# Adding the branches' results in accumulating transfers, and scaling two of three norms on VectorE, in a deformable-convolution block

## The chip, the core and the metric

The kernel runs on one core of one Trainium2 chip. The metric is the device time of one execution in microseconds (us). Three executions of the kernel before took 6637.6, 6637.77 and 6625.94 us; the median is 6637.6 us. Differences below some 0.2% (13 us) are not told from no change.

The engines are named as in the profile: PE is TensorE's matrix multiply and PEld its weight load, DVE is VectorE, ACT is ScalarE, POOL is GpSimd, SP is SyncE, which issues most of the transfers (DMAs). Each engine works through its own queue in order, and engines wait for one another by semaphores.

## What is computed

The input x is (2, 256, 128, 128) in fp32. Two layers follow each other: `x = x + layer0(groupnorm(x))`, then `x = x + layer1(groupnorm(x))`. Layer 1 is a 3x3 convolution with ternary weights and is not touched here. Layer 0 is this:

```python
def _branch(x, w_off, w_def, lw, lb, pad, dil):
    off = _conv(x, w_off, pad, dil)
    y = _deform_dw(x, off, w_def, pad, dil)       # 9 bilinear samples a pixel, depthwise
    return jax.nn.gelu(_ln2d(y, lw, lb), approximate=False)

x1 = _branch(x, off_w1, def_w1, bw1, bb1, 1, 1)
x2 = _branch(x, off_w2, def_w2, bw2, bb2, 9, 9)
x3 = _branch(x, off_w3, def_w3, bw3, bb3, 12, 12)
c = jnp.einsum('bchw,oc->bohw', x, conv_w[:, :, 0, 0]) + conv_b[None, :, None, None]
out = _ln2d(x1 + x2 + x3 + c, n1_w, n1_b)
h = out.transpose(0, 2, 3, 1)
h = jax.nn.gelu(h @ mlp_w1.T + mlp_b1, approximate=False) @ mlp_w2.T + mlp_b2
out = _ln2d(h.transpose(0, 3, 1, 2) + out, n2_w, n2_b)
```

`_ln2d` normalises each pixel over its 256 channels. There are three such norms on the way: the first in each of the three branches, with a Gelu behind it; the second over the sum of the branches; the third behind the MLP. The second and third have no function behind them.

## The kernel before

The kernel has three stages, one after the other. Stage A (to about 910 us) computes the offsets of all three branches and writes tables of x and of the samples' weights ("hats") to HBM. Stage B (to about 5830 us) takes the samples and runs all the rest of layer 0. Stage C is layer 1. The change lies in stage B alone.

**Sampling.** `sample_near` walks over 2 images x 66 row tiles x 3 branches, 396 units. For a unit, SP loads the hats `hy` and `hx` (line 1347, three buffers each) and table tiles `xs` (L1326), DVE multiplies the hats into a matrix `A` (L1367), PE multiplies it with the table tiles into PSUM `pm` (L1468, four buffers), ACT evicts `pm` into `ev` (L1480 and L1488, three buffers), and DVE adds `ev`, weighted per channel, into rings of rows (L1429, the first of a row by ACT at L1411). So each unit goes DVE, PE, ACT, DVE.

**The tail.** Four image rows (512 pixels) make a group; there are 64 groups, each in three branches, 192 chains. Once a branch's four rows are complete in its ring, its chain begins: `PixelTail.branch`, a generator. It yields a number of steps to pause; `Tail.advance` makes one step and lets every chain that is due emit its next instructions. Sampling calls `advance` twice for each unit and each half of the channels, some 1,580 times in all. So the tail's instructions are laid between those of the sampling by the count of steps, and the order on every engine is the order of emission. A yield has up to three values: the pause in steps; how many buffers the chain holds from then on; and whether the next piece is heavy for ACT (`True`: of the chains due with this mark, one goes on in a step). Buffers `v`, `other`, `xn`, `S`, `hT`, `xr` come from one pool of nine (`VBUFS`), of 512 KB each, and a chain is held back when the buffers would not do (`Tail.may`). At most four chains may be within a norm (`NORMS`).

A chain does this:

- All three branches: PE turns the ring's pixels into rows (L905, L913), ACT copies them into `v` (L921). `moments`: DVE takes mean and variance of each of four rows of 128x256 (L1101, L1103), adds a constant (L1105, L1106), POOL raises to the power -0.5 and multiplies (L1107, L1108) into `rs`. After seven steps `scaled` makes four ACTIVATEs on ACT (L1115), each `func(scale * row + bias)` in place, two in one step and two in the next; here with Gelu.
- Branch 0 then stores `v` to HBM, `g12d` (L1179, from SP). Branch 1 loads that into a second tile `other` (L1186), adds on DVE (L1189) and stores the sum (L1191). Branch 2 loads that (L1186), adds it on DVE (L1198), and goes on alone.
- Branch 2 loads x (`xn`), subtracts a mean on ACT (L1202), multiplies on PE by the 1x1 convolution's weights and adds on DVE (L1145). Second norm: `moments`, seven steps, `scaled` with Identity (L1115 again). Then PE turns the rows back (L1154), ACT copies into `S` (L1221), the MLP follows (matmuls L890 and L1137, Gelu L1230, addition L1145). Third norm: `moments`, seven steps, `scaled` with Identity. Turned back once more (L1154), DVE scales and adds x (L1254) and takes statistics for layer 1 (L1258), and SP stores the result (L1260).

All transfers of the chain are issued by SP, in the same queue as the loads of hats and tables. A DMA that waits for an engine keeps those behind it in that queue waiting too.

Of the kernel before, what the change touches and what calls it, by code (L numbers as in the profile page):

```python
# [13 lines left out]
AF = mybir.ActivationFunctionType  # L14
ALU = mybir.AluOpType
# [56 lines left out]
def conv_preact_kernel(ctx: ExitStack, tc: tile.TileContext, t: dict, out: bass.AP):  # L72
    nc = tc.nc
# [634 lines left out]
    with ExitStack() as actx:  # L708
        psum = actx.enter_context(tc.tile_pool(name="ps_a", bufs=1, space=PSUM))

        def gps():
# [4 lines left out]
        k = {  # L716
            "dxs": dxs,
            "zero": ap.tile([P, C], F32, name="zero"),
            "wz": ap.tile([P, KC, NZ], F32, name="wz"),
            "shift": ap.tile([P, len(dxs), P], F32, name="shift"),  # L720
            "mid": ap.tile([P, ZG, NOFF], F32, name="mid"),
            "hatw": ap.tile([P, 2, NTAP * NH], BF16, name="hatw"),
            "parts": [ap.tile([P, 2, ZG, P], BF16, name=f"parts{i}") for i in range(3)],
            "zr": ap.tile([P, ZRING, NZ], F32, name="zr"),
# [110 lines left out]
    class Tail:  # L835
# [135 lines left out]
        def branch(self, b, br, g, y):  # L971

            pin = self.pin
            cols = slice(g * NG, (g + 1) * NG)
            gv = g12d[b].rearrange("(k p) f -> p k f", p=P)[:, :, cols]
            z = []
            yield from self.normalised(z, y, (b, br, g))
            v = z[0]
            for c in range(KC):
                pin(  # L980
                    nc.scalar.activation(
                        v[:, c, :], z[1 + c], AF.Gelu,
                        scale=bw[:, br, c : c + 1], bias=bb[:, br, c : c + 1],
                    )
                )
            if br == 0:
                yield 2
                nc.sync.dma_start(gv, v)
                self.stored.add((b, br, g))
                return  # L990
            yield 1, 1 + br
            other = self.tile("other")
            while (b, br - 1, g) not in self.stored:
                yield 1
            nc.sync.dma_start(other, gv)
            if br == 1:
                yield 2
                pin(nc.vector.tensor_tensor(v, v, other, ALU.add))
                yield 2
                nc.sync.dma_start(gv, v)  # L1000
                self.stored.add((b, br, g))
                return
            xn = self.tile("xn")
            nc.sync.dma_start(xn, x[b].rearrange("(k p) h w -> p k (h w)", p=P)[:, :, cols])
            yield 4
            for c in range(KC):
                pin(
                    nc.scalar.activation(
                        xn[:, c, :], xn[:, c, :], AF.Identity, bias=negmean[b][:, c : c + 1]
                    )  # L1010
                )
            yield 1
            yield from self.finish(b, g, v, other, xn)
# [75 lines left out]
    class PixelTail(Tail):  # L1089
# [70 lines left out]
        def branch(self, b, br, g, y):  # L1160

            pin = self.pin
            gv = g12d[b].rearrange("c f -> (c f)").rearrange("(g p e) -> g p e", p=P, e=KC * NG)[g]
            xv = x[b].rearrange("(k p) h w -> p k (h w)", p=P)[:, :, g * NG : (g + 1) * NG]
            yield from self.entered()
            yield 0, 1, True
            v = self.tile("v")
            vf = v.rearrange("p k n -> p (k n)")
            vv = vf.rearrange("p (j c) -> p j c", c=C)
            rows = [vv[:, j, :] for j in range(NG // P)]  # L1170
            self.turned(vv, y, (b, br, g))
            self.read.add((b, br, g))
            rs = self.moments(rows)
            yield 7, min(1 + br, 2), True
            yield from self.scaled(rows, rs, AF.Gelu)
            self.norms -= 1
            if br == 0:
                yield 2
                nc.sync.dma_start(gv, vf)  # L1179
                self.stored.add((b, br, g))  # L1180
                return
            other = self.tile("other")
            of = other.rearrange("p k n -> p (k n)")
            while (b, br - 1, g) not in self.stored:
                yield 1
            nc.sync.dma_start(of, gv)  # L1186
            if br == 1:
                yield 2
                pin(nc.vector.tensor_tensor(vf, vf, of, ALU.add))  # L1189
                yield 2  # L1190
                nc.sync.dma_start(gv, vf)  # L1191
                self.stored.add((b, br, g))
                return
            yield 1, 3
            xn = self.tile("xn")
            nc.sync.dma_start(xn, xv)
            yield 2
            pin(nc.vector.tensor_tensor(vf, vf, of, ALU.add))  # L1198
            yield 2, 2, True
            for c in range(KC):  # L1200
                pin(
                    nc.scalar.activation(  # L1202
                        xn[:, c, :], xn[:, c, :], AF.Identity, bias=negmean[b][:, c : c + 1]
                    )
                )
            yield 1
            pairs = [(xn[:, c, :], convs[b][:, c, :]) for c in range(KC)]
            adds = [self.product("pc1", vv, convb3, pairs, h) for h in range(2)]
            yield 1, 1
            for add in adds:  # L1210
                add()
            yield 2
            yield from self.entered()
            rs = self.moments(rows)
            yield 7, None, True
            yield from self.scaled(rows, rs, AF.Identity)
            self.norms -= 1
            yield 2, 2, True
            S = self.tile("S")
            for c in range(KC):  # L1220
                pin(nc.scalar.copy(S[:, c, :], self.channels(rows, c)))  # L1221
            yield 1, 3
            hT = []
            for m in range(MC):
                if m % KC == 0:
                    hT.append(self.tile("hT"))
                hp = self.bank("hp")
                self.matmul(hp, [(w1[:, c, m * P : (m + 1) * P], S[:, c, :]) for c in range(KC)])
                pin(
                    nc.scalar.activation(  # L1230
                        hT[-1][:, m % KC, :], hp, AF.Gelu, bias=b1[:, m : m + 1]
                    )
                )
                yield 1, 4 if m < MC - 1 else 3
            pairs = [(hT[m // KC][:, m % KC, :], w2[:, m, :]) for m in range(MC)]
            add = self.product("h2", vv, b23, pairs, 0)
            yield 1, 3
            add()
            add = self.product("h2", vv, b23, pairs, 1)
            yield 1, 1  # L1240
            add()
            yield 2, 2
            yield from self.entered()
            rs = self.moments(rows)
            xr = self.tile("xr")
            nc.sync.dma_start(xr, xv)
            yield 7, None, True
            yield from self.scaled(rows, rs, AF.Identity)
            self.norms -= 1
            yield 2  # L1250
            for c in range(KC):
                zc = self.channels(rows, c)
                pin(
                    nc.vector.scalar_tensor_tensor(  # L1254
                        xr[:, c, :], zc, n2w[:, c : c + 1], xr[:, c, :], ALU.mult, ALU.add
                    )
                )
                pin(nc.vector.bn_stats(stats2[b][:, c, g, :], xr[:, c, :]))  # L1258
            yield 2, 1
            nc.sync.dma_start(  # L1260
                x1d[b].rearrange("(k p) f -> p k f", p=P)[:, :, g * NG : (g + 1) * NG], xr
            )
# [365 lines left out]
    with cmp.Else():  # L1628
        with ExitStack() as bctx:
            psum = bctx.enter_context(tc.tile_pool(name="ps_b", bufs=1, space=PSUM))  # L1630
            pool = bctx.enter_context(tc.tile_pool(name="bpool", bufs=1))
            k = {
                "A": [pool.tile([PX, 9, RI, WA], F32, name=f"A{i}") for i in range(2)],
            }
# [356 lines left out]
```

## Time and profile before

| what | value |
|---|---|
| median of three runs | 6637.6 us |
| the profiled execution | 6632.7 us, its span 6630.8 us |
| instructions in the trace | 100591 |
| PE busy | 6275.4 us, 95% of the span |
| PEld busy | 4993.0 us, 75% |
| DVE busy | 5906.2 us, 89% |
| ACT busy | 4189.3 us, 63% |
| POOL busy | 686.7 us, 10% |
| moved by DMA | 1360.49 MB, mean 205 GB/s |

"Busy" is the time in which at least one instruction of the engine runs. Instructions of one engine overlap at their ends, so a group's mean duration is longer than the time from one start to the next. A busy PE is not a PE at its peak. The costliest groups of stage B before, as the page has them: L1468 matmuls 3248.5 us for 17424 instructions, L1429 2481.2 us for 6372, L1480 1987.5 us for 4488, L1367 1009.5 us for 1124, L1107 on POOL 472.0 us for 320.

### The profile page before, as it was taken

The numbers are of one execution on the slowest core, as the hardware profiler recorded it, in microseconds if no ns is written. First come the engines' busy times: TensorE is split into PE (matmuls) and PEld (weight loads), VectorE is DVE, ScalarE is ACT, GpSimd is POOL, SyncE is SP. The second block draws the span as 40 slices with busy tenths as digits, with TensorE's granted clock in tenths as the row PEclk, the third lists the DMA queues.
The fourth block names the chain that finished last, engine by engine and source line by source line (L and its number), as shares of the span: only waits on it lengthen the run. The fifth ranks groups of instructions, "written<-read, shape, count | busy, mean of one in ns | idle before, by whom it ended". The sixth has DMA issues, their size and how long they took to land.

```text
span 6630.8 us, 100591 instructions
## 1 busy us (share of the span) xinstructions
PE 6275.4 (95%) x32242; PEld 4993.0 (75%) x32242; DVE 5906.2 (89%) x13772; ACT 4189.3 (63%) x8690; POOL 686.7 (10%) x665
## 2 busy tenths in 40 slices
PE   6899978999999999999999999999999999989999
PEld 3455558888888888888888888888888888734444
DVE  8766668999999999999778999999999999689996
ACT  2344447777777777777676777777777777554442
POOL 0000000111111111111110111111111111200000
PEclk9999978999999999999999999999999999989999
DMA  8976667877787777787667877788777777343332
GB/s 290 274 214 199 201 169 216 226 217 219 223 225 217 223 217 224 222 222 206 181 194 203 227 219 219 221 223 227 223 217 220 215 222 209 122 164 132 139 139 90
DMA packets 635795, 1360.49 MB, mean 205 GB/s; under 512 B 109592, under 2 KB 290344, under 8 KB 618736
## 3 DMA queue, kind: packets, MB, share of 16 engines
q1 hardware_dynamic: 617328, 1318.97, 68.9%
q10 hardware_dynamic: 17408, 33.56, 1.6%
q8 instruction: 261, 4.28, 0.3%
q14 instruction: 286, 2.34, 0.1%
q0 software_dynamic: 512, 1.34, 0.1%
HBM read 1087.10 MB, written 266.47 MB: 204 GB/s over the span
## 4 chain that ended last, share of the span: by engine, by line
PE 53%; DVE 30%; DMA 8%; ACT 5%; issue 3%; SPq 0%; POOL 0%; DVEq 0%; ACTq 0%; POOLq 0%
PE pm L1468 22%; DVE ring L1429 13%; PE pc L1810 6%; PE hp L890 6%; PE h L1137 5%; DVE A L1367 5%; PE pz L364 4%; DMA hx<-hats 3%; PE pc L1137 3%; DMA xa<-in_x 3%; ACT ev L1480 2%; ACT v L1115 2%; DVE st L1101 1%; PE ph L463 1%; PE tp L905 1%
## 5 line engine op out<-in xcount | busy, mean ns | idle before, releaser
L1468 PE MATMUL pm<-A,xs 96*128 96x216 f32 (+2 forms) x17424 | 3248.5, 343 | 176.4 <-ACT ev L1480 45.4
L1468 PEld LDWEIGHTS pm<-A,xs 96*128 96x128 f32 x17424 | 3049.1, 195 | 374.1 <-ACT ev L1480 119.2
L1429 DVE SCALAR_TENSOR_TENSOR ring<-ev,defw,ring 128x256 f32<-128x256 f32 (+4 forms) x6372 | 2481.2, 451 | 98.1 <-ACT ev L1480 47.8
L1480 ACT COPY ev<-pm 128x432 f32<-128x432 f32 (+4 forms) x4488 | 1987.5, 483 | 869.3 <-PE pm L1468 695.8
L1367 DVE TENSOR_TENSOR A<-hy,hx 96x768 f32<-96x768 f32 (+1 forms) x1124 | 1009.5, 945 | 164.1 <-DMA hx<-hats 89.8
L1107 POOL TENSOR_TENSOR rs<-rs,mhalf 128x4 f32<-128x4 f32 x320 | 472.0, 1475 | 4202.5 <-DVE rs L1106 3543.9
L1810 PE MATMUL pc<-cring,signs 128*128 128x512 bf16 x3456 | 757.9, 382 | 17.0 <-ACT cring L1727 7.4
L1115 ACT ACTIVATE v<-v,rs 128x256 f32<-128x256 f32 x1280 | 694.4, 594 | 16.7 <-POOL rs L1108 16.6
L1810 PEld LDWEIGHTS <-signs 128*128 128x128 bf16 x3456 | 339.6, 98 | 434.6 <-issue 27.7
L890 PE MATMUL hp<-S,w 128*128 128x512 f32 x1024 | 493.9, 607 | 0.8 <-ACT S L1221 0.8
L364 PE MATMUL pz<-wz,xa 128*128 128x486 f32 x1024 | 461.6, 578 | 25.3 <-DVE zr L371 25.3
L1137 PE MATMUL h<-w,hT 128*128 128x256 f32 x2048 | 477.1, 379 | 0.0
L1101 DVE BATCH_NORM_STATS2 st<-v 128x6 f32<-128x256 f32 x1280 | 446.9, 410 | 30.8 <-ACT v L921 30.8
L1411 ACT ACTIVATE ring<-ev,defw 128x256 f32<-128x256 f32 (+1 forms) x856 | 404.5, 485 | 24.2
L1137 PEld LDWEIGHTS h<-w,hT 128*128 128x128 f32 x2048 | 369.3, 190 | 65.5 <-issue 1.0
L364 PEld LDWEIGHTS pz<-wz,xa 128*128 128x128 f32 x1024 | 189.2, 191 | 189.3 <-issue 126.1
L921 ACT COPY v<-tp 128x512 f32<-128x512 f32 x384 | 207.8, 598 | 182.7 <-PE tp L913 182.4
L1230 ACT ACTIVATE hT<-hp,b 128x512 f32<-128x512 f32 x256 | 176.1, 688 | 218.6 <-PE hp L890 214.6
L890 PEld LDWEIGHTS hp<-S,w 128*128 128x128 f32 x1024 | 196.7, 197 | 139.4 <-issue 121.3
L470 ACT ACTIVATE hb<-ph 96x512 f32<-96x512 f32 (+1 forms) x384 | 209.8, 596 | 144.2 <-PE ph L463 135.6
L1137 PE MATMUL pc<-convw,xn 128*128 128x256 f32 x1024 | 271.1, 393 | 2.4 <-ACT xn L1202 2.4
L371 ACT COPY zr<-pz 128x486 f32<-128x486 f32 x128 | 72.1, 564 | 256.5 <-PE pz L364 253.8
(246 smaller groups left out, 5132.5 us busy)
## 6 DMA issues: line engine op xcount, KB each, us to landing
hy<-hats SPq DMA_DIRECT2D x1112, 288.0 KB
hx<-hats SPq DMA_DIRECT2D x1112, 288.0 KB
xs<-tables SPq DMA_DIRECT2D x1452, 96.0 KB
g12d<-v SPq DMA_DIRECT2D x128, 512.0 KB
other<-g12d SPq DMA_DIRECT2D x128, 512.0 KB
hats<-hb SPq DMA_DIRECT2D x64, 720.0 KB
hats<-hb SPq DMA_DIRECT2D x64, 576.0 KB
xa<-in_x ACTq DMA_DIRECT2D x64, 512.0 KB
```

The lines of the kernel that those rows point to most:

```text
L364: nc.tensor.matmul(pz[:, 0:NZ], lhsT=xt[:, c, r, :], rhs=k["wz"][:, c, :], start=c == 0, stop=c == KC - 1,)
L890: nc.tensor.matmul(out, lhsT=w, rhs=v, start=i == 0, stop=i == n - 1)
L1101: pin(nc.vector.bn_stats(st[:, j, :], rows[j]))
L1107: nc.gpsimd.tensor_tensor(rs[:, 0, :], rs[:, 0, :], mhalf[:, 0:n], ALU.pow)
L1115: nc.scalar.activation(row, row, func, scale=rs[:, 0, j : j + 1], bias=rs[:, 1, j : j + 1])
L1137: nc.tensor.matmul(bank[:, j, :], lhsT=v[:, px], rhs=w, start=False, stop=i == len(pairs) - 1,)
L1367: nc.vector.tensor_tensor(dst, hy[:, i0:i1].rearrange("p i t w -> p t i w"), hx[:, i0:i1].rearrange("p i t w -> p t i w"), ALU.mult,)
L1411: pin(nc.scalar.mul(dst, src, w))
L1429: pin(nc.vector.scalar_tensor_tensor(dst, src, w, dst, ALU.mult, ALU.add))
L1468: nc.tensor.matmul(pv[:, j, :, m0:m1, :], lhsT=xts[b, Rt][t][:, c * P : (c + 1) * P], rhs=A[:, y0:y1, m0:m1, AO + t * CI : AO + (t + 1) * CI],
L1480: nc.scalar.copy(dst.rearrange("p m (t j) -> p t m j", j=CI), pm[:, 0 : len(ts), 0:n].rearrange("p t (m j) -> p t m j", j=CI),)
L1810: nc.tensor.matmul(pc, lhsT=signs[:, k, (h * 3 + t) * 3 + kx, m * P : (m + 1) * P], rhs=xc[:, i, k, t * JC : (t + 1) * JC, kx : kx + W], s ...
```

## The change

Branch 1 no longer loads, adds and stores: it issues one transfer from POOL that adds `v` to what lies in HBM. Branch 2 issues one transfer from POOL that adds what lies in HBM to `v` in SBUF. The two DVE additions, the tile `other` and its loads are gone. The first norm keeps its ACTIVATEs with Gelu; the four ACTIVATEs of the second and of the third norm become four `tensor_scalar` on DVE (multiply by one value for each pixel, add another), in one step and without the mark for ACT. The pauses and the numbers of held buffers are set accordingly.

```diff
             rs = self.moments(rows)
-            yield 7, min(1 + br, 2), True
+            yield 7, 1, True
             yield from self.scaled(rows, rs, AF.Gelu)
             self.norms -= 1
...
-            other = self.tile("other")
-            of = other.rearrange("p k n -> p (k n)")
             while (b, br - 1, g) not in self.stored:
                 yield 1
-            nc.sync.dma_start(of, gv)
             if br == 1:
-                yield 2
-                pin(nc.vector.tensor_tensor(vf, vf, of, ALU.add))
-                yield 2
-                nc.sync.dma_start(gv, vf)
+                nc.gpsimd.dma_start(gv, vf, accum_op=ALU.add)
                 self.stored.add((b, br, g))
                 return
-            yield 1, 3
+            nc.gpsimd.dma_start(vf, gv, accum_op=ALU.add)
+            yield 1, 2
             xn = self.tile("xn")
             nc.sync.dma_start(xn, xv)
-            yield 2
-            pin(nc.vector.tensor_tensor(vf, vf, of, ALU.add))
-            yield 2, 2, True
+            yield 4, 2, True
...
             rs = self.moments(rows)
-            yield 7, None, True
-            yield from self.scaled(rows, rs, AF.Identity)
+            yield 7
+            for j, row in enumerate(rows):
+                pin(
+                    nc.vector.tensor_scalar(
+                        row, row, rs[:, 0, j : j + 1], rs[:, 1, j : j + 1], ALU.mult, ALU.add
+                    )
+                )
             self.norms -= 1
```

The last hunk stands twice, for the second and for the third norm.

More of the change, by code (lines that the diff above doesn't have):

```diff
@@ L1246, in branch @@
             nc.sync.dma_start(xr, xv)
-            yield 7, None, True
-            yield from self.scaled(rows, rs, AF.Identity)
+            yield 7
+            for j, row in enumerate(rows):
+                pin(
+                    nc.vector.tensor_scalar(
+                        row, row, rs[:, 0, j : j + 1], rs[:, 1, j : j + 1], ALU.mult, ALU.add
+                    )
+                )
             self.norms -= 1
```

## The prediction

> **What bounds the kernel now.** I read the slices first, then the chain of waits, then the waits and windows of the middle stage, last the groups that the diff touches.
>
> ```profile
> PE   6899978999999999999999999999999999989999
> DVE  8766668999999999999778999999999999689996
> ACT  2344447777777777777676777777777777554442
> DMA  8976667877787777787667877788777777343332
> PE 53%; DVE 30%; DMA 8%; ACT 5%; issue 3%; SPq 0%; POOL 0%; DVEq 0%; ACTq 0%; POOLq 0%
> ```
>
> Rows of digits: one slice is 166 us; last row: the chain that ended last, by engine. The change lies in slices 6 to 34, where the samples are taken (the first L1468 matmul starts at 920 us, the last L1429 ends at 5704 us: 4785 us). There PE and DVE are both at 9, ACT at 7. The windows, columns PE, weight loads, DVE, ACT, POOL, then clock, DMA share and GB/s:
>
> ```profile
> 2000.00:2500.00 500.00, 489.61 (x2590) 433.93 (x2589) 479.11 (x1215) 364.55 (x797) 68.58 (x67) 0.99 0.79 220
> 4000.00:4500.00 500.00, 489.73 (x2614) 434.38 (x2614) 484.36 (x1232) 365.59 (x801) 73.18 (x68) 1.00 0.80 223
> ```
>
> PE works 98% of the time, DVE 96%, ACT 73%. So two engines bound the stage by turns, with 2 to 4% between them. The chain of waits, followed through the stage, gives the turns: PE about 2530 us, DVE 1470 (31%), ACT 320, DMA 320. A turn of ACT looks like this (start, length, what):
>
> ```profile
> 2052.81 0.52 ACT ev L1480
> 2053.32 0.99 ACT v L1115 x2
> 2054.31 1.25 ACT ev L1480 x3
> ...
> 2056.29 0.98 ACT v L1115 x2
> 2057.27 1.05 ACT ev L1480 x3
> 2058.32 1.00 ACT v L1115 x2
> 2059.32 0.41 ACT ev L1480
> ```
>
> The reader is to see that the norms' scalings (L1115) stand in front of the evictions L1480 for which PE waits: pairs of ACTIVATE of 0.99 us delay PE by as much.
>
> [...] the 128x1024 additions took 1.22 us, the 120x1536 tensor_scalar L474 0.95. [...] The trace has no accumulating transfer.
>
> **The change part by part.** The built order of instructions shows it done as told: 128 accumulating DMAs on POOL, 256 fewer DMAs on SP, two DVE additions per group gone, 512 tensor_scalars in, 512 ACTIVATEs out; the MLP's matmuls come one step (5 to 17 L1468 matmuls) earlier, the order is otherwise kept. I price from these rows (group: busy us, mean ns; then starts on DVE):
>
> ```profile
> L1115 ACT ACTIVATE v<-v,rs 128x256 f32<-128x256 f32 x1280 | 694.4, 594 | 16.7 <-POOL rs L1108 16.6
> L1189 DVE TENSOR_TENSOR v<-v,other 128x1024 f32<-128x1024 f32 x64 | 77.9, 1218 | 2.0 <-DMA other<-g12d 1.9 <-issue 0.2
> L1198 DVE TENSOR_TENSOR v<-v,other 128x1024 f32<-128x1024 f32 x64 | 77.7, 1214 | 0.0
> L251 DVE TENSOR_SCALAR dn<-wk,q_pr,q_nc 128x256 f32<-128x256 f32 x18 | 7.3, 406 | 0.1
> ...
> 104.24 0.40 DVE L249 TENSOR_SCALAR sg<-wk,q_pr,q_er 128x256 bf16<-128x256 f32 x1
> 104.56 0.41 DVE L251 TENSOR_SCALAR dn<-wk,q_pr,q_nc 128x256 f32<-128x256 f32 x1
> 104.89 0.60 DVE L423 COPY offs<-po 128x432 f32<-128x432 f32 x1
> ```
>
> *Additions out (DVE).* Neighbours overlap, so I count from start to start: the addition at 2010.85 us is followed at 2011.98, 1.13 us. 128 x 1.13 = 145 us off DVE. The chain's pieces for L1189 and L1198 sum to 11 + 15 = 26 us; so 26 on the path.
>
> *Scalings in (DVE).* L251 is the same form with two pointer scalars: 0.41 us, and 0.325 from start to start (104.24, 104.56, 104.89). 512 x 0.325 = 166 us; if none overlap 512 x 0.406 = 208. DVE is on the path for 31% of the stage, so 166 x 0.31 = 51 us on the path. Bounds: half of it (26) if DVE's 4% idle takes the rest; 208 if DVE became the bound throughout. Net DVE load: +21 us (to +63).
>
> *Scalings out (ACT).* 0.99 us for two: 512 x 0.495 = 253 us off ACT. The chain holds 110 us of L1115 in this stage; by number 512 of 1280 are those that go (44 us); matching the pieces with the program's order gives 64. I take 64. Bounds: 0 if PE has no more to give, since its idle time in the stage that names ACT is 45 + 42 + 33 = 120 us (L1480, the S copies L1221, L1488); 120 if all of that goes.
>
> *Wait of the scaling.* It waits on DVE for POOL's rs, and behind it stand the L1429 that PE's buffers wait for. Moments are issued seven steps ahead: some 1,580 steps in 4785 us are 3.0 us each, so 21 us. From L1106 to the end of L1108 it took 2.7 us (median), 6.3 at most. Margin 15 us: nothing.
>
> *Transfers.* SP loses 192 issues net of the 64 first stores: 128 loads (0.53 us) and 64 stores (0.33), 89 us of issue, and the wait that stood in its queue:
>
> ```profile
> SPq L1191 <- DVE v L1189: 389.1, 60, 13.5
> SPq L1186 <- PE h L1137: 147.2, 29, 6.9
> DVE A L1367 <- DMA hx<-hats: 89.8, 54, 13.3
> ```
>
> Behind these queue the hats and tables; but most hats wait for DVE's builds (L1367) anyway, issued after L1189, and only 23 us of the chain are SP's own. I take 5 us. POOL gets 128 issues and, in front of later rs, the wait for the Gelu and for the earlier transfer. The nearest row, an indirect DMA of POOL, took 0.95 us: 128 us on an engine that is 14% busy; hidden by the 15 us margin. Bytes: before 256 transfers of 512 KB (134 MB, 13% of 220 GB/s x 4785 us); after 64 plain and 128 accumulating. At the price of a plain transfer each, 25% less of 13%; at twice[...], 25% more: DMA load -3% to +3%, on 320 us of DMA turns about 10 us either way. I take 0. The result is needed seven steps (21 us) after its issue, against 4.0 to 9.6 us to landing of POOL's transfers here.
>
> *Buffers.* The second tile (other) is no longer held, so chains may start earlier; gain 0 to 10, I take 0. The drain after 5705 us is PE-bound (110 of 125 us busy) and its matmul order is unchanged: 0.
>
> **Sum.** Taken off the path 26 + 64 + 5 = 95; of removed pieces I count 0.8, since another engine's turn is close behind (76); added 51. Result -25 us. The profiled execution took 6632.7 us (span 6630.8 and 1.9 around): 6608. The median of the runs is 4.9 above it: 6613 us.
>
> **Rivals.**
> 1. *More than that* (0.12): ACT's bursts were what kept PE from running ahead, and with them all 120 us of PE's waits for ACT and the full DVE removal come: about -90, 6548. For: ACT's pairs sit between evictions. Against: ACT waits 696 us for PE at L1480; it is often idle first.
> 2. *Hidden* (0.17): PE at 98% has nothing to give, the DVE work nearly cancels (+21 us x 0.31 = 7): 6638 to 6645.
> 3. *VectorE becomes the bound* (0.13, the slower side): each scaling takes 0.41 us without overlap[...], and DVE's net +63 us counts nearly in full, while ACT's relief buys nothing: +30 to +63, about 6690. It decides once DVE's idle in the steady windows falls from 4% to under 2% with PE's rising.
> 4. *Accumulating transfers cost a multiple* (0.08): at four times a plain one, 64 + 512 = 576 units against 256, DMA share 0.79 to 0.95; the hats come late, and 320 us of DMA turns grow by half: +100 to +160, 6760.
>
> That the change does something else is ruled out by the built order.
>
> **How the numbers follow.** The forecast has 0.50 (own range 6575 to 6628), the rivals 0.12, 0.17, 0.13 and 0.08. A measurement here tells no less than 0.2% (13 us) from no change. Faster by more: 0.50 + 0.12 less 0.02 for the forecast's near edge = 0.60; within: 0.17, some of rival 2's upper end lost and the edge gained, 0.18; slower: 0.22. The range leaves out half of rival 1 (0.06), rival 4 (0.08) and the upper end of rival 3 (0.05): 6560 to 6685.
>
> **What would show it.** ACT's share in windows 2000 to 2500 falls from 73% to about 68%; DVE's stays at 96 to 97%; tensor_scalar rows of 0.40 us, 512 of them; no wait of DVE for POOL above a few us; L1115 on the chain falls from 2% to about 1%. Wrong if scalings last over 0.5 us, if DVE waits for the accumulating transfers at L1145, or if the DMA share rises above 0.85.

## The result, and the profile after

The changed kernel took 7035.8 us, median of five runs (7021.75 to 7042.38), against 6637.8 us for the kernel before (five runs): 1.0599 times as long, 95% interval 1.0585 to 1.0613. The forecast was 6613 us, faster by 0.4%. Its profiled execution has a span of 7034.0 us.

From the page of the changed kernel, the slices (here one is 176 us):

```profile
PE   5899978899999999999998999999999999879999
...
DVE  7866668888898888888768888888988988679997
ACT  2344456666666666666556666666666666535443
...
DMA  8966678777777777777558777777777777433332
```

VectorE, ScalarE and the DMA engines each lose about a tenth in the middle stage, TensorE keeps its nine. Only GpSimd became busier, with 12% of the span in place of 10%; so none of them became the bound. The windows of the same kernel, with the columns of the windows before (PE, weight loads, DVE, ACT, POOL, clock, DMA share, GB/s), give the amount:

```profile
2000.00:2500.00 500.00, 466.28 (x2400) 411.68 (x2399) 447.28 (x1159) 322.39 (x690) 83.09 (x72) 0.96 0.75 197
4500.00:5000.00 500.00, 465.62 (x2392) 409.97 (x2391) 441.54 (x1144) 318.93 (x681) 84.40 (x73) 0.97 0.74 197
```

TensorE fell from 98% to 93%, VectorE from 96% to 89%, and the granted clock from 0.99 or 1.00 to 0.96 or 0.97. Two engines that both idle more may be waiting for each other. The table of waits, TensorE's rows first and VectorE's next, names where:

```profile
PE zc L1154 <- DVE v L1248: 242.2, 63, 5.9
...
PE zc L1154 <- issue: 60.8, 27, 5.4
...
PE zc L1154 <- PE pm L1471: 14.7, 22, 1.0
...
DVE A L1370 <- PE pm L1471: 370.7, 67, 8.5
```

Columns: who waits, on which line, for whom, then us in total, times, longest. (Line numbers below the change move by a few from kernel to kernel: L1468 of before is L1471 here, L1367 is L1370, L1429 is L1432. L1248 and L1211 are the new scalings of the third and the second norm; L1154, the transposes behind both, keeps its number.) The same two places in the kernel before, from its groups and its waits:

```profile
L1154 PE MATMUL zc<-ident,v 128*128 128x128 f32 x1024 | 141.0, 280 | 12.4 <-ACT v L1115 10.0 <-DVE st L1101 2.3
...
DVE A L1367 <- PE pm L1468: 72.9, 55, 4.6
```

TensorE waits 318 us ahead of the transposes; before, it was 12.4 us. VectorE writes each `A` into one of two buffers and waits until TensorE has read what stood there; this wait grew from 72.9 to 370.7 us. So TensorE's standstill comes back to VectorE.

One such wait, in the timeline of the changed kernel (start, length, engine, what; in brackets the idle time before it):

```profile
2629.79 10.81 PE L1471 MATMUL pm<-A,xs 96*128 96x216 f32 x59
...
2636.45 2.69 DVE L1370 TENSOR_TENSOR A<-hy,hx 96x768 f32<-96x768 f32 x3
...
2639.07 3.12 DVE L1432 SCALAR_TENSOR_TENSOR ring<-ev,defw,ring 128x256 f32<-128x256 f32 x8
...
2642.11 1.40 DVE L1101 BATCH_NORM_STATS2 st<-v 128x6 f32<-128x256 f32 x4
...
2644.04 1.38 DVE L1248 TENSOR_SCALAR v<-v,rs 128x256 f32<-128x256 f32 x4
...
2644.59 2.21 PE L1154 MATMUL zc<-ident,v 128*128 128x128 f32 x8 [4.00 <-DVE v L1248]
```

TensorE ends its matmuls at 2640.6 and comes to the transposes. The scalings that they need stand on VectorE behind work that was emitted ahead of them, and start 3.4 us later. Nothing is wrong with the scalings: `rs` is there (VectorE's idle time ahead of L1248 is 0.2 us in all, none ahead of L1211), and four of them take 1.38 us. They are late because VectorE is late: it adds up what TensorE has multiplied and ScalarE has evicted, so in the order of emission it runs several us behind TensorE. In the kernel before, nothing that TensorE reads two steps later was made by VectorE at this place.

### The profile page after: what moved, and what is told of

Read it like the earlier page. It is cut to its first block, busy times and chain, and to the rows that moved or that the text cites. A ratio compares the mean times of both kernels' runs of the same rounds, so it can differ in the third digit from the quotient of the medians.

```text
span 7034.0 us, 100037 instructions
## 1 busy us (share of the span) xinstructions
PE 6437.9 (92%) x32242; PEld 5105.3 (73%) x32242; DVE 5933.5 (84%) x14156; ACT 4019.2 (57%) x8178; POOL 868.5 (12%) x793
## 5 line engine op out<-in xcount | busy, mean ns | idle before, releaser
L1471 PE MATMUL pm<-A,xs 96*128 96x216 f32 (+2 forms) x17424 | 3291.6, 347 | 99.5 <-ACT ev L1483 29.7
L1471 PEld LDWEIGHTS pm<-A,xs 96*128 96x128 f32 x17424 | 3131.9, 199 | 264.3 <-issue 112.7
L1483 ACT COPY ev<-pm 128x432 f32<-128x432 f32 (+4 forms) x4488 | 2044.4, 481 | 1438.9 <-PE pm L1471 1286.6
L1432 DVE SCALAR_TENSOR_TENSOR ring<-ev,defw,ring 128x256 f32<-128x256 f32 (+4 forms) x6372 | 2481.9, 451 | 121.7 <-ACT ring L1414 47.8
L1370 DVE TENSOR_TENSOR A<-hy,hx 96x768 f32<-96x768 f32 (+1 forms) x1124 | 1014.5, 944 | 515.6 <-PE pm L1471 370.7
L1154 PE MATMUL zc<-ident,v 128*128 128x128 f32 x1024 | 246.0, 368 | 318.3 <-DVE v L1248 242.2
L1154 PEld LDWEIGHTS zc<-ident,v 128*128 128x128 f32 x1024 | 154.9, 173 | 409.0 <-issue 329.3
L1115 ACT ACTIVATE v<-v,rs 128x256 f32<-128x256 f32 x768 | 416.0, 592 | 0.0
```

What stands on the lines that cost most here:

```text
L1115: nc.scalar.activation(row, row, func, scale=rs[:, 0, j : j + 1], bias=rs[:, 1, j : j + 1])
L1370: nc.vector.tensor_tensor(dst, hy[:, i0:i1].rearrange("p i t w -> p t i w"), hx[:, i0:i1].rearrange("p i t w -> p t i w"), ALU.mult,)
L1432: pin(nc.vector.scalar_tensor_tensor(dst, src, w, dst, ALU.mult, ALU.add))
L1471: nc.tensor.matmul(pv[:, j, :, m0:m1, :], lhsT=xts[b, Rt][t][:, c * P : (c + 1) * P], rhs=A[:, y0:y1, m0:m1, AO + t * CI : AO + (t + 1) * CI],
L1483: nc.scalar.copy(dst.rearrange("p m (t j) -> p t m j", j=CI), pm[:, 0 : len(ts), 0:n].rearrange("p t (m j) -> p t m j", j=CI),)
```

## The experiments

All ratios are to the kernel before, run beside it on the same chip, with 95% intervals; idle and busy times are those of one profiled execution. Three theories stood against each other: TensorE waits for VectorE's lag at the transposes (first); the accumulating transfers or GpSimd's queue cost the time (second); the added load makes VectorE the bound (third, the prediction's rival 3).

### One part of the change at a time

*Accumulating transfers alone*: the changed kernel, with both norms scaled by ScalarE as before.

```diff
-            yield 7
-            for j, row in enumerate(rows):
-                pin(nc.vector.tensor_scalar(row, row, ...))
+            yield 7, None, True
+            yield from self.scaled(rows, rs, AF.Identity)
```

> The kernel before with the accumulating transfers alone; both norms are still scaled on ACT. If PE's wait for the scalings on DVE is the cause (first theory), this is between 25 us faster than before and equal to it: 6610 to 6640 us. If POOL's queue or the transfers are the cause (second theory), it is near the changed kernel: 6900 to 7040 us. If more load on DVE is the cause (third theory), it is faster by what the additions had on the chain, about 26 us: 6612 us.

Measured: 6611.2 us, 0.9963 [0.9948, 0.9978], as the first and the third theory have it. *Scalings alone*: the kernel before, with this diff turned round in both norms and the additions left on VectorE.

> The kernel before with the scalings of the second and third norm on DVE alone; loads, additions and stores of the branches as before. First theory: PE waits 5 to 6.5 us for each of 64 groups, 320 to 420 us: 6960 to 7060 us. Second theory: about as before, 6600 to 6650. Third theory (DVE load): 166 us of DVE more and nothing less, so even slower than the changed kernel, by some 145 us: near 7180.

Measured: 7200.7 us, 1.0852 [1.0832, 1.0871]. This is above the range of the first theory and near the number of the third, so the time alone doesn't decide between them. The groups do; from those of the first and then of the second run (busy us, mean ns, idle before):

```profile
L1154 PE MATMUL zc<-ident,v 128*128 128x128 f32 x1024 | 141.6, 279 | 11.6 <-ACT v L1115 11.2 <-DVE xr L1247 0.2
```
```profile
L1154 PE MATMUL zc<-ident,v 128*128 128x128 f32 x1024 | 257.2, 397 | 436.1 <-DVE v L1255 314.7 <-DVE v L1218 121.4
```

The transfers are exonerated: by themselves they make the kernel 0.4% faster. The whole loss is the scalings', and most of it sits in front of and inside the transposes. Between the changed kernel and the transfers alone there are 410 us of span (7034.0 - 6623.9). TensorE's idle time ahead of L1154 gives 307 of them (318.3 - 11.6), the transposes themselves 104 (246.0 - 141.6 us busy), the sampling matmuls 58 (3291.6 - 3233.4), and their own idle time gives back 63 (162.6 - 99.5): 406. The longer busy time of the transposes is in part waiting too: in the wait shown above the first four of the eight start 0.24 to 0.33 us apart, as one row after another is scaled, and the last four 0.21 us apart.

The scalings alone cost still more than the whole change. Of the 161 us of span between the two (7195.5 - 7034.0), 118 are TensorE's idle time ahead of L1154 (436.1 - 318.3), and VectorE was busy for only 88% of the steady windows, so this too is the wait and not a bound by VectorE. With the additions on VectorE its lag may be longer; no run shows that.

### The distance to the reader, and one norm at a time

*Later transposes*: four steps in place of two between the scalings and the transposes, in both norms.

```diff
-            yield 2, 2, True
+            yield 4, 2, True
...
-            yield 2
+            yield 4
```

> The changed kernel with two more steps (6 us) between the scalings on DVE and the transposes on PE that read them, in both norms; no work is added or taken away. First theory: the wait of 4.0 us behind the third norm and of 1.1 us behind the second go, PE's time in front of L1154 falls from 303 us to under 60, and the time is 6590 to 6680 us. Second and third theory: unchanged, 7000 to 7060 us.

*Second norm alone* on VectorE, the third back on ScalarE:

> The changed kernel with the third norm scaled on ACT again; only the second is on DVE. If each norm's wait stood alone, 242 us of 303 would go: about 6780 us. If the wait is DVE's lag behind PE, and is taken by whichever norm comes next (first theory, as the lag in the trace of before says: 4.5 us at the second norm, 1.3 at the third), the second norm takes it: 64 x 4.5 = 290 us, 6900 us. Third theory (DVE load): 83 us of DVE less, 6950 us.

*Third norm alone* on VectorE:

> The changed kernel with the second norm's scaling back on ScalarE with its old pauses; the third norm's stays on VectorE. First theory, as it stands after the run with the second norm alone on VectorE (there the second norm took the whole wait, 334 us): the wait is one lag of VectorE behind TensorE in a group, which shows at whichever norm is on VectorE; TensorE idle ahead of the third norm's transposes 250 to 350 us, time 6950 to 7060. If the two norms had each a loss of its own: the third alone about 250 us idle, and the time 6611 + 300 = about 6900. Theory of VectorE's load: half the scalings, half the loss, about 6820.

| run | median us | ratio | TensorE idle ahead of L1154 |
|---|---|---|---|
| changed kernel | 7035.8 | 1.0599 [1.0585, 1.0613] | 318.3 us |
| four steps | 6772.0 | 1.0207 [1.0190, 1.0224] | 162.4 us |
| second norm alone | 7051.4 | 1.0629 [1.0611, 1.0647] | 333.9 us |
| third norm alone | 6956.0 | 1.0483 [1.0465, 1.0501] | 340.3 us |

Two steps more of distance take away some 260 us (1.0599 - 1.0207 = 3.9%) without touching a single instruction's work, which the theory of load can't give. They don't take away all, as was expected (idle time under 60 us, 6590 to 6680 us); what was left is found below. And the loss doesn't halve with half the scalings: either norm alone takes the whole wait of some 335 us. For the second norm alone the time came out 151 us above the 6900 us of the first theory; the third alone met its range. The likely reading is that TensorE runs ahead of VectorE once in a group, and the first place where it has to read from VectorE's queue brings the two level. In the changed kernel the second norm's transposes took 76 us of the wait and the third's 242; with the second alone all of it falls there. With the scalings alone, though, the two norms wait for 121 and 315 us, more than one such wait. In the run with the second norm alone the table of waits calls it something else:

```profile
PE zc L1154 <- issue: 330.6, 58, 7.4
```

"Issue" stands for a wait that the profile can't put down to anybody. It vanishes with the scalings (11.6 us in the run with the transfers alone), and in these 58 waits TensorE starts 0.10 us after the end of the group's first scaling on VectorE: it is the same wait. A reader who trusts the label only would look for it in vain.

### The wait without the work, and the work without the wait

*Wait alone*: both norms scaled by ScalarE, and behind each scaling VectorE multiplies one column of the row by 1.0. The output is the same; the transposes now depend on VectorE's queue for 512 instructions of 0.14 us.

```diff
             yield from self.scaled(rows, rs, AF.Identity)
+            for row in rows:
+                pin(nc.vector.tensor_scalar(row[:, 0:1], row[:, 0:1], 1.0, None, ALU.mult))
             self.norms -= 1
```

> Accumulating transfers, both norms' scalings on ScalarE as before, and behind them four VectorE multiplications of one column (128x1) by 1.0 for each norm, 512 in all: the output is the same, VectorE gets next to no work (512 x about 0.1 us = 50 us), but TensorE's transposes now wait for VectorE's queue. First theory (the wait costs, not the work): TensorE idle ahead of L1154 200 to 420 us, time 6850 to 7050. Theory of VectorE's load: at most 50 us more than the 6611 of the accumulating transfers alone, 6610 to 6660.

*Work alone*: ScalarE scales, and VectorE makes 512 multiply-adds of 128x240 from one half of a spare buffer into the other, which nobody reads.

```diff
             yield from self.scaled(rows, rs, AF.Identity)
+            for j in range(len(rows)):
+                pin(
+                    nc.vector.tensor_scalar(
+                        self.spare[:, 1], self.spare[:, 0], rs[:, 0, j : j + 1],
+                        rs[:, 1, j : j + 1], ALU.mult, ALU.add,
+                    )
+                )
             self.norms -= 1
```

> Accumulating transfers, both norms' scalings on ScalarE as before, and beside them 512 VectorE multiply-adds of nearly the same size (128x240 fp32 in place of 128x256, two pointer scalars) from a spare buffer into a spare buffer that nobody reads: the work of the scalings on VectorE without a consumer. First theory: no wait at L1154 (below 30 us), time 6611 plus VectorE's share on the path, 20 to 100 us: 6630 to 6710. Theory of VectorE's load: near the changed kernel's time, 6950 to 7050.

Measured: the wait alone 7122.4 us, 1.0737 [1.0719, 1.0756]; the work alone 6681.6 us, 1.0068 [1.0045, 1.0091]. The table of waits of the first:

```profile
PE zc L1154 <- DVE v L1245: 248.5, 59, 7.7
PE zc L1154 <- DVE v L1211: 128.6, 27, 7.4
```

and the groups of the second, the transposes and the idle work:

```profile
L1154 PE MATMUL zc<-ident,v 128*128 128x128 f32 x1024 | 141.7, 280 | 12.3 <-ACT v L1115 11.0 <-ACT hT L1230 1.0
L1251 DVE TENSOR_SCALAR spare<-spare,rs 128x240 f32<-128x240 f32 x256 | 103.6, 405 | 8.5 <-POOL rs L1108 1.4
```

This pair settles it between wait and load. 43 us of VectorE's work with a reader (21.8 + 21.1) cost more than the change did; 206 us of it (103.6 + 102.9) without a reader cost 70 us (1.0068 - 0.9963 = 1.05% of 6632), and nothing at the transposes. The wait alone costs more than the whole change and lies 72 us above the range expected. In part that fits: there ScalarE keeps its own scalings, and the relief of it (measured below) is missing. But the idle time ahead of the transposes is longer too, 433 us against 318, and no run takes that apart.

### Where the lead comes from matters

If distance is what is missing, it could also come from the other side. *Earlier scalings*: three steps behind the moments in place of seven, six ahead of the transposes in place of two.

```diff
-            yield 7
+            yield 3
...
-            yield 2, 2, True
+            yield 6, 2, True
```

> The changed kernel with the pauses around the VectorE scalings moved: the scalings are issued 3 steps behind the moments in place of 7, and 6 steps ahead of the transposes in place of 2, in both norms (total 9 as before). First theory (TensorE waits at the transposes L1154 because VectorE reaches the scaling some 1 to 8 us behind it; the lead of 2 steps, about 6 us less VectorE's own lag, was too short): with 4 steps (12 us) more of lead nearly all of it goes. TensorE idle ahead of L1154 below 60 us (318 in the changed kernel, 162 with a lead of 4), transposes near 141 us busy, time 6590 to 6680. Theory of VectorE's load (the 166 us of scalings make VectorE the bound): the load is as in the changed kernel, so the time stays near 7036, or at least near the 6772 of the lead of 4. Wait for POOL's values (the margin ahead of the scaling gets shorter, 9 us in place of 21): VectorE would wait at L1211 and L1248 for POOL, over 50 us.

Measured: 6809.3 us, 1.0265 [1.0248, 1.0282]. The expectation was met at the transposes (idle 4.7 us) and missed in the time, by 129 us from the far edge. The wait had a new place; from the table of waits of this run:

```profile
PE pm L1471 <- DVE A L1370: 165.1, 66, 4.6
```

and one of the 66 in its timeline:

```profile
2605.28 0.74 DVE L1257 SCALAR_TENSOR_TENSOR xr<-zc,n2w,xr 128x512 f32<-128x512 f32 x1
...
2606.06 0.69 DVE L1261 BATCH_NORM_STATS2 stats<-xr 128x6 f32<-128x512 f32 x1
2606.67 0.73 DVE L1257 SCALAR_TENSOR_TENSOR xr<-zc,n2w,xr 128x512 f32<-128x512 f32 x1
...
2607.44 0.70 DVE L1261 BATCH_NORM_STATS2 stats<-xr 128x6 f32<-128x512 f32 x1
...
2608.05 1.37 DVE L1211 TENSOR_SCALAR v<-v,rs 128x256 f32<-128x256 f32 x4
...
2609.33 2.69 DVE L1370 TENSOR_TENSOR A<-hy,hx 96x768 f32<-96x768 f32 x3
...
2612.16 2.26 PE L1471 MATMUL pm<-A,xs 96*128 96x144 f32 x6 [3.05 <-DVE A L1370]
```

The output of the group ahead (L1257 and L1261, twice) and the second norm's scalings of the next group fell into one step: 4.1 us of VectorE's work in a row in front of the `A` that TensorE needs next. A chain's scaling and the previous chain's output stand a group apart, so the sum of the later pauses decides whether they meet. With four and four steps they met as well: 55 of the 64 scalings of the second norm stood directly behind L1261, and there the remaining wait fell (156 of 162 us). This is what the run with four steps had left.

So two kernels were made in which they don't meet, by a longer third lead. *Apart*: leads of four and six, the scalings seven steps behind the moments.

```diff
-            yield 2, 2, True
+            yield 4, 2, True
...
-            yield 2
+            yield 6
```

> The changed kernel with leads of 4 steps in the second norm and of 6 in the third (2 and 2 in the changed kernel, 4 and 4 in the run that stood at 6772). With 4 and 4 the second norm's scalings stood on VectorE right behind the previous group's output (2 x L1257 and L1261, 2.9 us in one step) and TensorE waited 156 us for them; the longer third lead moves that output two steps behind the scalings. Theory of the burst (two chains' VectorE work in one step is what is left of the wait): TensorE idle ahead of L1154 below 50 us, time 6600 to 6680. If VectorE's lag alone needs more than 4 steps in the second norm: idle stays near 150 us, time near 6770. Theory of VectorE's load: near 6770 as well, with VectorE busy 96% or more in the steady windows.

*Early and apart*: three steps behind the moments, leads of six and eight.

> The changed kernel with the scalings 3 steps behind the moments, leads of 6 in the second norm and of 8 in the third. With 6 and 6 (6809) nothing waited at the transposes any more, but TensorE waited 165 us in 66 waits for the next A (L1370), which stood on VectorE behind the output of the previous group and the scalings. Theory of the burst: with the output two steps away the waits for A fall below 70 us and the time to 6640 to 6720. If the scalings alone delay A (their 1.4 us in one step is enough): waits for A stay over 130 us, time near 6800.

*Third late*: the second norm on ScalarE, the third on VectorE with a lead of six.

> Second norm's scaling on ScalarE, third norm's on VectorE with a lead of 6 steps in place of 2 (6956 with 2). First theory: the wait at the third norm's transposes goes (337 us, below 30), and with it TensorE's slow matmuls behind each wait; what is left is half of VectorE's added work (35 us) less half of ScalarE's relief: 6590 to 6660, about the accumulating transfers alone (6611). If a lead does not help but only moves the wait to A (as with 6 and 6): waits for A over 100 us and a time over 6700.

| run | median us | ratio | idle ahead of L1154 | TensorE's wait for A |
|---|---|---|---|---|
| four and four | 6772.0 | 1.0207 [1.0190, 1.0224] | 162.4 | 30.9 |
| four and six, apart | 6555.9 | 0.9869 [0.9848, 0.9889] | 25.1 | 27.2 |
| six and six, early | 6809.3 | 1.0265 [1.0248, 1.0282] | 4.7 | 165.1 |
| six and eight, early and apart | 6571.6 | 0.9895 [0.9878, 0.9913] | 5.6 | 29.2 |
| third alone, six | 6595.6 | 0.9938 [0.9923, 0.9953] | 12.7 | 17.6 |

In "apart" 2 of the 64 scalings of the second norm stand directly behind L1261, in "early and apart" 1, against 55 and 58 in the runs that they mend. Both kernels beat the kernel before and the changed one, "apart" by 1.3% and 7%; the burst is shown in both places. They came out 44 and 68 us below the near edges expected, probably since these took ScalarE's relief as small; the next run measures it. For the third norm alone a lead of six takes the wait from 340 to 13 us and the time from 6956 to 6596 us, inside the range expected. The windows of "apart":

```profile
2000.00:2500.00 500.00, 496.37 (x2650) 441.17 (x2649) 491.86 (x1282) 351.01 (x761) 67.82 (x81) 1.00 0.83 218
4500.00:5000.00 500.00, 496.53 (x2656) 442.82 (x2655) 491.29 (x1278) 352.73 (x764) 67.75 (x81) 1.00 0.81 218
```

TensorE 99%, VectorE 98%, at full clock: this is what the change looks like when nobody waits.

### What ScalarE's relief is worth

*Relief alone*: the transfers, and no scaling of the second and third norm by anybody. The kernel leaves that work out, so its output is not the function's; the second mark for ScalarE in each norm goes with it.

```diff
-            yield from self.scaled(rows, rs, AF.Identity)
+            yield 1
```

> Accumulating transfers, and no scaling at all in the second and third norm (both are left out; the statistics are still made): ScalarE has 512 ACTIVATEs less and VectorE nothing more. It measures what the relief of ScalarE is worth by itself, which the prediction put at 64 us on the path (bounds 0 and 120). If that size was right: 6611 - 64 = about 6547, 6530 to 6570. If the relief is hidden, since TensorE and VectorE are the bound: 6595 to 6615. If ScalarE's bursts were the hidden bound: below 6500. With the 70 us that the same work costs on VectorE (the run with the work alone), the move can only pay if this run stands more than 70 us below 6611.

Measured: 6477.1 us, 0.9762 [0.9744, 0.9780]. This is below 6500, where the expectation put ScalarE's bursts as a hidden bound. The relief is 2.01% (0.9963 - 0.9762), 133 us, twice what the prediction took; with the two intervals it is 118 to 149 us, so it reaches or passes the bound of 120 that was set. Of 148 us of span against the run with the transfers alone, TensorE's idle time gives 71 (340.5 to 269.7, span less busy) and its busy time 78 (6283.4 to 6205.7): the matmuls' busy time was stretched too.

The terms add up: 0.9963 for the transfers, less 0.0201 for the relief, plus 0.0105 for the work on VectorE make 0.9867; "apart" measured 0.9869. Each term has an interval of some 0.002 to either side, so that the sum meets the measurement this closely is luck; that it meets it within some 0.4% is not.

## Why the prediction was wrong

*Wait of the scaling* is the step that failed: "Moments are issued seven steps ahead ... Margin 15 us: nothing." The margin was worked out on one side only, from the moments to the scaling, and there it held: with even three steps VectorE waited for POOL's `rs` only 4.0 us over the whole run (2.7 at L1248, 1.3 at L1211). The sentence named what is queued behind the waiting scaling on VectorE; it did not ask who reads what the scaling makes. That is TensorE, two steps or 6 us later by the prediction's own 3.0 us a step, less VectorE's lag. When ScalarE made it, that was enough (12.4 us of wait in all): ScalarE evicts right behind the matmuls, for which it waited 696 us at L1480 of the kernel before. VectorE comes one stage later.

The lag could have been worked out blind, by laying the built order beside the trace of before: when TensorE came to the place of each transposition there, and when VectorE had worked off everything ahead of the scaling that it needs. VectorE was later by a median of 4.5 us (second norm) and 1.3 us (third), summed over 64 groups 336 and 84 us: 420 us, less what is made good when one wait brings both level. The two together showed 318. The split came out the other way, 76 us at the second norm and 242 at the third, so the lag gives the rough size of the wait and not its place.

The other steps:

- *Additions out* and *SP's queue*: 26 + 5 us, times 0.8, make 25; measured 0.37% of 6632 or 25 us, give or take 10. Right as a sum; no run tells its parts from one another. ("256 fewer DMAs on SP" is 192, as the prediction itself counts further down; nothing rests on it.) In one of SP's waits for L1189 in the kernel before it issued nothing from 2006.3 to 2012.1 us, then the store and, behind it, six loads of hats. VectorE lost 138 us of busy time (5906.2 to 5768.4) against the 145 worked out.
- *Transfers on POOL* at nothing: within that sum, right, and rival 4 falls. An issue took 0.93 and 0.92 us (0.95 taken), landing 8.4 and 9.5 us in the run with the transfers alone, within the 21 us that they had; the DMA share in its steady windows was 0.80, against 0.79 before. "At twice" was the better of the two prices: in the changed kernel a packet of 4 KB took 364 ns on average in the queue of the accumulating transfers and 165 ns in that of the plain ones.
- *Scalings in*: each 0.407 us, four in 1.38, as priced. On the path 51 us were taken; the work alone cost 70 (52 to 88 with the two intervals) with a width of 240 in place of 256. If anything a little small, within the bounds. Beside GpSimd's work the scalings were no slower: 230 of the 512 ran while POOL was computing and took 0.403 to 0.414 us, the others 0.396 to 0.416. None of them ran during one of POOL's 128 issues of transfers, so for these the changed kernel shows nothing.
- *Scalings out*: 64 us taken, 133 measured, twice as much and at or beyond the upper bound of 120. That bound was TensorE's idle time that names ScalarE. It didn't bound this relief, as more than half came out of TensorE's busy time (78 of 148 us). Rival 1's mechanism, ScalarE's bursts holding TensorE up, was at work after all, covered by the wait: TensorE's idle time ahead of the sampling matmuls that names ScalarE's evictions (of `pm` and into `S`) is 99.5 us with the transfers alone and 38.5 with the relief.
- *Buffers* and *drain* at nothing: no run took them apart.
- *Rival 3*, VectorE as the bound, had the right engine and the wrong reason. Its own sign, VectorE's idle time under 2%, came true in the fast kernel (98% busy) and not in the slow one (89%).

So the work that the change moves is worth 25 + 133 - 70 = 88 us of gain, and "apart" has it (1.31% of 6643, 87 us). What made it a loss of 398 us, far outside the range of 6560 to 6685, is a wait that none of the prediction's rivals held.

Of its signs, ScalarE's share fell further than foretold (64% for 68) and VectorE's fell to 89% where 96 to 97 were foretold; the rows of 0.40 us, the missing wait for POOL and the low DMA share came true. None of the signs looked at TensorE's transposes.

## What to carry to other kernels

When work moves to another engine, ask on both sides: whether its inputs are there, and who reads its result, how long after, measured in that engine's own place in the order. An engine that works behind another by a few us, as VectorE did here behind TensorE (a median of 4.5 us at the second norm and 1.3 at the third), is the wrong place for that other's inputs, unless the lead is lengthened by the lag; the lag can be read from the trace of before. And when pauses are changed, look at what falls into the same step: here 4.1 us in a row on a nearly full engine cost 238 us (6809 against 6572), half of the 480 us that lie between the changed kernel and "apart".

## What the runs showed of the hardware

In this kernel a wait of TensorE cost more than its length. Windows of the changed kernel around the wait shown above (first the length, then the columns as before):

```profile
2636.00:2640.00 4.00, 4.00 (x22) 3.70 (x22) 4.00 (x7) 3.83 (x11) 0.93 (x1) 1.00 0.96 193
2640.00:2644.50 4.50, 0.60 (x4) 0.26 (x2) 4.39 (x18) 1.04 (x3) 0.34 (x1) 0.79 0.97 256
2644.50:2648.00 3.50, 3.40 (x12) 3.01 (x13) 3.46 (x12) 0.00 (x0) 3.26 (x2) 0.50 1.04 265
2648.00:2652.00 4.00, 4.00 (x19) 3.89 (x19) 3.86 (x7) 2.60 (x6) 0.00 (x0) 0.82 0.48 119
2652.00:2656.00 4.00, 4.00 (x24) 4.00 (x23) 4.00 (x9) 3.22 (x8) 0.00 (x0) 1.00 0.78 247
```

The granted clock (third value from the end) falls to 0.50 behind a wait of 4 us and is back at 1.00 for good in the window that begins 7.4 us after the work goes on. The clock's records hold only the values 0.5 and 1.0, so the means 0.79 and 0.82 put its fall about 2 us after the matmuls' end (0.42 x 4.5 us at half speed in the second window) and its return about 5 us after they go on (0.36 x 4 us in the fourth). The stretch at half clock between the two is 6.8 us long. Shorter waits did it too: while the samples are taken, 4 of the 5 waits of 2.0 to 2.5 us in the changed kernel and all 4 in the kernel before were followed by half clock. In the same stage half clock adds up to 534 us in the changed kernel and to 225 us in the kernel before.

Over the whole run of the changed kernel, sampling matmuls that follow each other directly stand a median 257 ns apart in the first 5 us behind a wait of over 1.5 us (1,066 of them), and 182 ns otherwise. Added up over the first 6 us, what lies above 182 ns comes to 110 us in the changed kernel and 45 us in the kernel before. So some 65 us of the loss are slow matmuls and not waits; this is also why the sampling matmuls' busy time grew, from 3248.5 to 3291.6 us, with nothing changed in them. The transposes were slower as well: the last four of the eight above start 0.21 us apart, against 0.11 us in the run "six and six, early", where nothing holds them up.
